# Four layers of graph attention on one core: layer 3's row totals from weights added up in pairs on VectorE

## The chip, the core and the metric

The kernel runs on one core of a Trainium2 chip. A core has five engines, each with an instruction stream of its own that it works through in order: TensorE (PE: matrix products and transposes, results in PSUM), VectorE (DVE), ScalarE (ACT), GpSimd (POOL) and SyncE (SP, which issues transfers). [...] The metric is the time of one execution on the device in microseconds (us), the median of the runs.

## The reference, cut to what matters

Sixteen batches of 1024 nodes with 256 features go through four layers of graph attention. Each layer begins with a normalisation and a relu and adds its result to x.

```python
h = jnp.maximum(_layernorm(x, axis=-1), 0.0)      # (x - mean) / sqrt(var), then relu
x = x + _L3_gnn_ref(h, adj, ...)                  # layers 0, 1, 2 in the same way

def _L3_gnn_ref(nodes_embed, node_adj, W, a_src, a_dst, bias, ln_gamma, ln_beta):
    h = jnp.einsum('bnd,hde->bhne', nodes_embed, W)            # H=4 heads of 64 features
    ...                                  # weight[i,j] = e_src[i] + e_dst[j] where there is an edge
    weight = jax.nn.leaky_relu(weight, negative_slope=0.01)
    weight = jnp.where(node_adj[:, None] == 0, NEG, weight)
    attention = jax.nn.softmax(weight, axis=-1)
    dst = jnp.einsum('bhij,bhje->bhie', attention, h) + bias[None, :, None, :]
    out = jax.nn.relu(dst) + h
    ...                                  # each head is normalised over its 64 features
```

A softmax is a sum of weights times values, divided by the total of the weights. The kernel makes the exponentials as products of one factor for the target i and one for the source j, so a weight is the larger (or smaller) of two such products, times the mask. Common factors of i cancel in the quotient. In layer 3 a factor q[j] is kept out of the weights and lies in the values: the values are q[j] h[j], and the total is the sum over j of q[j] w[j,i].

## The kernel before

The source nodes j lie in NI = 8 blocks of 128 on the partitions, the 1024 targets in the free dimension. Weights are made on VectorE, one instruction for one block of sources, from a row in PSUM (the same on all partitions), a factor of j for each partition and the mask:

```python
def weigh(b, turn, c, op, into):
    while row_taken:                    # one row in PSUM, shared by the two streams
        yield 0.25
    row_taken.append(b)
    r = psum.tile([P, N], F32, name="row", bufs=1)
    for i in range(NI):
        turn(r[:, ts(i, P)], i)         # TensorE makes the row
    yield 0.5
    for j in range(NI):
        w = edges.tile([P, N], F32, name=f"weights{b % 2}")      # 8 buffers for each stream
        nc.vector.scalar_tensor_tensor(w, r, c(j), masks[b][:, j // 2, :, j % 2], op0=op, op1=ALU.mult)
        into.append(w)
        ...
        yield 0.5
```

Layers 0 to 2 take their products from these weights as 128x257 matmuls (values and total together, L461). In layer 3 a head has only 64 features, and the weights are the moving operand: four matmuls of 32 columns, one on each quarter of the array, run side by side as a group.

```python
def in_tiles(parts, accT, first, last):
    for n, (values, moving) in enumerate(parts):
        ...
        made = nc.tensor.matmul(accT[ts(n, QUAD), :], values, moving, start=first, stop=last)   # L586

def add_values(h, j):                   # 2 groups of four: blocks j+1 and j
    for n in (j + 1, j):
        parts = [(V3[:, n, h, ts(e, QUAD)], moving) for moving in halves_of(h, n) for e in range(2)]
        in_tiles(parts, acc, n == 3, n == NI - 4)

def add_totals(h, j):                   # 1 group of four for the two blocks
    parts = [
        (V3[:, j + n, h, E:].to_broadcast([P, QUAD]), halves_of(h, j + n)[g])
        for g, n in ((0, 1), (0, 0), (1, 1), (1, 0))
    ]
    in_tiles(parts, total, j == 2, j == NI - 4)

for h in range(H):
    acc, total = accumulator(b), accumulator(b)
    ...                                 # head 0: the values first, then a transpose for the rows of heads 1 to 3
    behind = weigh3(h + 1)              # the next head's weights are made behind this head's products
    yield from start(behind, b)
    for first in range(0, NI, 4):       # a chunk is four blocks
        pinned = []
        for j in (first + 2, first):
            add_totals(h, j)
            if h > 0:
                add_values(h, j)
        for _ in range(4):
            next(behind, None)
        yield 1.8 if h == 0 else 5.4
    ...                                 # copies of acc and total, transposes, division, bias, relu, normalisation
```

Before each layer's projection two blocks of x are centered and cut at zero, on VectorE, and their squares are summed on ScalarE:

```python
def center_by_sums(xb, minus_mean, pair, centered):
    for n in range(2):
        nc.vector.tensor_scalar(                                 # L302
            centered[:, n, :], xb[:, 2 * pair + n, :], minus_mean[:, n : n + 1], 0.0,
            op0=ALU.add, op1=ALU.max,
        )
    ...
```

Two streams, of the even and the odd batches, are interleaved. A generator yields a virtual length for each of its steps, the stream that is behind goes on, and stream 1 starts LAG = 111 later, so that layer 3 of one stream is issued beside earlier layers of the other:

```python
streams = [[0.0, stream(0)], [LAG, stream(1)]]
while streams:
    ahead = min(streams, key=lambda s: s[0])
    t = next(ahead[1], None)
    ...
    ahead[0] += t
```

Of the kernel before, what the change touches and what calls it, by code (L numbers as in the profile page):

```python
# [32 lines left out]
F32 = mybir.dt.float32  # L33
BF = mybir.dt.bfloat16
# [4 lines left out]
ALU = mybir.AluOpType  # L39
# [22 lines left out]
def short_path(ctx: ExitStack, tc: tile.TileContext, ins: dict, out: bass.AP, bad: bass.AP):  # L62
# [233 lines left out]
    def accumulator(b: int) -> bass.AP:  # L296
        return psum.tile([P, HALF], F32, name=f"acc{b % 2}")

    def center_by_sums(xb: bass.AP, minus_mean: bass.AP, pair: int, centered: bass.AP) -> bass.AP:

        for n in range(2):
            nc.vector.tensor_scalar(  # L302
                centered[:, n, :], xb[:, 2 * pair + n, :], minus_mean[:, n : n + 1], 0.0,
                op0=ALU.add, op1=ALU.max,
            )
        squared = small.tile([P, 2], F32, name="squared")
        for n in range(2):
            square = work.tile([P, D], BF, name="square", bufs=1)
            nc.scalar.activation(  # L309
                square, xb[:, 2 * pair + n, :], AF.Square, bias=minus_mean[:, n : n + 1],  # L310
                accum_out=squared[:, n : n + 1],
            )
        return inverse_root(squared, 2, D, LN_EPS)

    def project(b: int, l: int, xb: bass.AP, sums: bass.AP, pair: int, evict):


        centered = work.tile([P, 2, D], F32, name="centered", bufs=3)
        if sums is None:
            mv = small.tile([P, 2, nc.vector.BN_AGGR_DIM], F32, name="mv", bufs=2)  # L320
            for n in range(2):
                stats = small.tile([P, nc.vector.BN_STATS_DIM], F32, name="stats", bufs=1)
                nc.vector.bn_stats(stats, xb[:, 2 * pair + n, :])
                nc.vector.bn_aggr(mv[:, n, :], stats)
                nc.vector.tensor_scalar(  # L325
                    centered[:, n, :], xb[:, 2 * pair + n, :], mv[:, n, 0:1], 0.0,
                    op0=ALU.subtract, op1=ALU.max,
                )
            rstd = inverse_root(mv[:, :, 1], 2, D, LN_EPS, D)
        else:  # L330
            minus_mean = small.tile([P, 2], F32, name="minus_mean")
            nc.vector.tensor_scalar_mul(minus_mean, sums[:, ts(pair, 2)], -1.0 / D)  # L332
            rstd = center_by_sums(xb, minus_mean, pair, centered)
        yield 0.5
        turned = psum.tile([P, NK, 2 * P], F32, name="misc")
        for n in range(2):
            for k in range(NK):
                nc.tensor.transpose(turned[:, k, ts(n, P)], centered[:, n, ts(k, P)], ident)  # L338
        hT = wide.tile([P, NK, 2 * P], F32, name="hT", bufs=3)
        nc.scalar.mul(hT, turned, ROOT_D)  # L340
        yield 1.0
        for n in range(2):
            projected = accumulator(b)[:, : D + EXT[l]]
            for k in range(NK):
                nc.tensor.matmul(  # L345
                    projected, hT[:, k, ts(n, P)], W[l][:, k, :],
                    start=(k == 0), stop=(k == NK - 1),
                )
            evict(2 * pair + n, projected, rstd[:, n : n + 1])
        yield 2.5  # L350
# [50 lines left out]
    def batch(b: int):  # L401
# [130 lines left out]


        h3, ex = last["h3"], last["ex"]
        y = single.tile([P, NI, H, E], F32, name="y")
        normed = []

        def center(h: int, blocks=slice(0, NI), engine=nc.gpsimd):
# [19 lines left out]
        def rescale(yh: bass.AP, blocks, head, rstd: bass.AP, engine=nc.gpsimd):  # L558
            shape = list(yh.shape)
            nc.vector.tensor_mul(yh, yh, rstd.unsqueeze(2).to_broadcast(shape))  # L560
            engine.tensor_mul(yh, yh, gamma[:, head].unsqueeze(1).to_broadcast(shape))
            engine.tensor_add(yh, yh, xb[:, blocks, head])

        weights = []

# [37 lines left out]
                ]  # L603
                in_tiles(parts, acc, n == 3, n == NI - 4)

        def add_totals(h: int, j: int):

            parts = [
                (V3[:, j + n, h, E:].to_broadcast([P, QUAD]), halves_of(h, j + n)[g])
                for g, n in ((0, 1), (0, 0), (1, 1), (1, 0))  # L610
            ]
            in_tiles(parts, total, j == 2, j == NI - 4)

        behind = weigh3(0)
        yield from start(behind, b)

        rest = small.tile([P, NI, H], F32, name="rest", bufs=1)
        nc.gpsimd.tensor_scalar_mul(rest, ex[:, :, 2 * H :], THIRDS)
# [2 lines left out]
        nc.gpsimd.tensor_sub(rest, rest, thirds[:, 0])  # L621
        nc.gpsimd.tensor_copy(thirds[:, 1], rest)
        nc.gpsimd.tensor_sub(thirds[:, 2], rest, thirds[:, 1])
        for h in range(H):


            acc = accumulator(b)
            total = accumulator(b)
            if h == 0:
                for first in range(0, NI, 4):  # L630
                    for _ in range(4):
                        next(behind)
                    pinned = []
                    for j in (first + 2, first):
                        add_values(h, j)
                    yield 3.6
                for _ in behind:
                    pass
                turned_thirds = psum.tile([3 * QUAD, P], BF, name="misc")
                made = nc.tensor.transpose(  # L640
                    turned_thirds, thirds.rearrange("p t i h -> p (t i h)"), ident_bf
                )
                tc.keep_in_program_order(made)
                thirds_T = small.tile([3 * QUAD, P], BF, name="thirds_T", bufs=1)
                nc.scalar.copy(thirds_T, turned_thirds)
            behind = weigh3(h + 1)
            yield from start(behind, b)

            for first in range(0, NI, 4):
                pinned = []  # L650
                for j in (first + 2, first):
                    add_totals(h, j)
                    if h > 0:
                        add_values(h, j)
                for _ in range(4):
                    next(behind, None)
                yield 1.8 if h == 0 else 5.4
            for _ in behind:
                pass
            copies = []  # L660
            for accT in (acc, total) if h == 0 else (total, acc):
                copies.append(wide.tile([P, HALF], F32, name="sums"))
                nc.scalar.copy(copies[-1], accT)  # L663
                next(testing)
                next(coming, None)
            sums, totals = copies if h == 0 else copies[::-1]
            yield 0.5
            turned = psum.tile([P, NG, P], F32, name="misc")
            for i in range(NG):
# [14 lines left out]
                inv.unsqueeze(3).to_broadcast([P, NH, NG, E]),  # L684
            )
            yield 0.5
            if h > 0:
                rescale(*normed.pop())


# [2 lines left out]
            elif h < H - 1:  # L693
                normed.append(center(h, engine=nc.gpsimd if h < H - 2 else nc.vector))
            else:
                normed += [center(h, slice(g * NG, g * NG + NG), nc.vector) for g in range(NH)]
            yield 1.0
        for _ in coming:
            pass
        while normed:  # L700
            rescale(*normed.pop(0), engine=nc.vector if len(normed) == 0 and b == B - 1 else nc.gpsimd)
        for g in range(NH):
            queue = nc.gpsimd if b < B - 1 else (nc.sync, nc.scalar)[g]
            queue.dma_start(
                in_blocks(out[b, ts(g, HALF), :]),
                y[:, ts(g, NG)].rearrange("p (c t) h e -> p c t (h e)", t=2),
            )
        yield 1.0

# [395 lines left out]
```

## Time and profile before

The median is 2933.43 us (three runs, 2932.9 to 2933.43). The profiled execution has a span of 2931.4 us with a granted TensorE clock of 0.995.

| group (line, engine) | count | busy us | mean ns |
|---|---|---|---|
| L461 TensorE, products of layers 0 to 2 | 6144 records | 1435.6 | 384 |
| L586 TensorE, layer 3's values and totals | 6144 records | 691.7 | 596 |
| L345 TensorE, projections | 2048 records | 516.1 | 389 |
| L367 VectorE, weights of layer 3 | 512 | 629.0 | 1272 |
| L367 VectorE, weights of layers 0 to 2 | 384 | 473.7 | 1273 |
| L302 VectorE, relu(x - mean) | 504 | 195.7 | 416 |
| L393 ScalarE, exponential of 128x256 | 256 | 121.1 | 473 |

An fp32 matmul leaves two records, so 6144 records are 3072 matmuls. The four matmuls of a group run side by side, so the busy time of L586 is less than the sum of its records. A busy share is the mean over the whole span. Windows split the span into stretches and give each engine's busy time in each. A line that a group of instructions has in the profile is the line of the helper that issues them.

### The profile page before, as it was taken

Reading aid. Unit: us, or ns where it says so; the run is one execution under the profiler, and the core shown is the slowest. Engines: PE = TensorE matmul, PEld = TensorE weight load, DVE = VectorE, ACT = ScalarE, POOL = GpSimd, SP = SyncE. Lnnn points to the kernel's source line nnn. Section 1 sums busy time; section 2 is a strip of 40 time slices with the busy share of each in tenths; the row PEclk is TensorE's granted clock in tenths of the full one; section 3 lists DMA queues with packets and bytes.
Section 4 is the critical chain, followed back from the end, with each engine's and each line's share of the span. In section 5 each row is a group of like instructions: output and inputs, shape, how many; then the busy total and the mean of one; then the engine's idle time right before and its main releaser. Section 6 shows DMA issues by size and latency. Waiting matters only on the chain.

```text
span 2931.4 us, 44756 instructions
## 1 busy us (share of the span) xinstructions
PE 2810.0 (96%) x16790; PEld 1961.9 (67%) x16790; DVE 2147.9 (73%) x4490; ACT 1088.2 (37%) x3010; POOL 981.3 (33%) x1533
## 2 busy tenths in 40 slices
PE   7999999999999999999999999999999999999986
PEld 5775857668576685766758577685766857667552
DVE  5658688586976859778586885868768587685857
ACT  1333434343343433424334343433434334343332
POOL 2123324243242423424233242432424224242333
PEclk9999999999999999999999999999999999999998
DMA  8204022030321303122031220303203031110101
GB/s 126 39 8 65 30 30 58 8 51 29 37 51 16 56 17 51 37 29 59 1 51 37 30 58 8 51 30 37 51 12 47 29 49 39 15 30 1 22 22 31
DMA packets 127967, 106.14 MB, mean 36 GB/s; under 512 B 79872, under 2 KB 98432, under 8 KB 127744
## 3 DMA queue, kind: packets, MB, share of 16 engines
q0 software_dynamic: 47328, 66.10, 15.4%
q1 hardware_dynamic: 79568, 35.53, 5.4%
q8 instruction: 135, 2.21, 0.3%
q10 hardware_dynamic: 848, 1.57, 0.2%
q14 instruction: 88, 0.72, 0.1%
HBM read 153.49 MB, written 33.55 MB: 64 GB/s over the span
## 4 chain that ended last, share of the span: by engine, by line
PE 59%; DVE 26%; issue 8%; POOL 3%; ACT 3%; DMA 0%; POOLq 0%; ACTq 0%; SPq 0%; DVEq 0%
PE acc L461 36%; DVE weights L367 16%; PE acc L586 10%; PE acc L345 9%; PE misc L338 2%; DVE centered L302 2%; POOL rstd L293 2%; DVE V L417 1%; PE row L374 1%; POOL y L544 1%; DVE y L545 1%; DVE var L555 1%; ACT square L309 1%; DVE y L551 1%; DVE mean L549 1%
## 5 line engine op out<-in xcount | busy, mean ns | idle before, releaser
L461 PE MATMUL acc<-V,weights 128*128 128x257 f32 x6144 | 1435.6, 384 | 33.5 <-DVE weights L367 15.7
L461 PEld LDWEIGHTS acc<-V,weights 128*128 128x128 f32 x6144 | 1136.6, 190 | 281.9 <-DVE weights L367 75.3
L586 PE MATMUL acc<-weights,V 128*32 128x512 f32 x6144 | 691.7, 596 | 12.0 <-DVE weights L367 8.1
L367 DVE SCALAR_TENSOR_TENSOR weights<-row,ex,mask 128x1024 f32<-128x1024 f32 x512 | 629.0, 1272 | 97.3 <-PE row L574 65.8
L345 PE MATMUL acc<-W,hT 128*128 128x259 f32 (+1 forms) x2048 | 516.1, 389 | 38.1 <-ACT hT L340 26.9
L367 DVE SCALAR_TENSOR_TENSOR weights<-row,V,mask 128x1024 f32<-128x1024 f32 x384 | 473.7, 1273 | 0.8 <-PE row L374 0.8
L345 PEld LDWEIGHTS acc<-W,hT 128*128 128x128 f32 x2048 | 378.7, 190 | 135.1 <-ACT hT L340 44.4
L586 PEld LDWEIGHTS acc<-weights,V 128*32 128x32 f32 x6144 | 189.1, 110 | 417.7 <-issue 410.3
L393 ACT ACTIVATE below<-acc,inv 128x256 f32<-128x256 f32 x256 | 121.1, 473 | 813.1 <-DVE inv L386 569.6
L293 POOL TENSOR_TENSOR rstd<-rstd,minus_half 128x2 f32<-128x2 f32 (+1 forms) x321 | 292.8, 912 | 20.3
L309 ACT ACTIVATE square<-x_b,minus_mean 128x256 bf16<-128x256 f32 x504 | 255.7, 507 | 110.3 <-DVE minus_mean L332 105.3
L441 POOL TENSOR_TENSOR x_b<-x_b,beta 128x256 f32<-128x256 f32 x128 | 93.5, 731 | 488.6 <-ACT square L309 483.5
L292 POOL TENSOR_SCALAR rstd<-squared 128x2 f32<-128x2 f32 x252 | 80.0, 317 | 464.0 <-ACT square L309 451.0
L385 DVE TENSOR_SCALAR inv<-acc 128x1 f32<-128x1 f32 x256 | 39.1, 153 | 255.3 <-PE acc L461 254.0
L302 DVE TENSOR_SCALAR centered<-x_b,minus_mean 128x256 f32<-128x256 f32 x504 | 195.7, 416 | 5.1
L340 ACT ACTIVATE hT<-misc 128x512 f32<-128x512 f32 x256 | 150.2, 592 | 129.6 <-PE misc L338 129.3
L396 DVE SCALAR_TENSOR_TENSOR x_b<-below,x_b 128x256 f32<-128x256 f32 x256 | 131.8, 515 | 84.9 <-ACT below L393 83.0
L663 ACT COPY sums<-acc 128x512 f32<-128x512 f32 x128 | 74.9, 585 | 308.6 <-PE acc L586 301.0
L413 ACT ACTIVATE V<-acc,rstd 128x3 f32<-128x3 f32 x384 | 98.4, 261 | 231.1 <-PE acc L345 230.6
L417 DVE TENSOR_SCALAR V<-acc,rstd,V 128x256 f32<-128x256 f32 x256 | 131.4, 537 | 59.8 <-ACT V L413 58.9
L338 PE MATMUL misc<-ident,centered 128*128 128x128 f32 x1024 | 158.7, 277 | 13.7 <-DVE centered L325 11.5
L170 POOL DMA_DIRECT2D adj_i<-in_adj_dram x128 | 74.4, 582 | 290.1 <-ACT adj_i L175 248.8
(96 smaller groups left out, 2212.8 us busy)
## 6 DMA issues: line engine op xcount, KB each, us to landing
adj_i<-in_adj_dram POOLq DMA_DIRECT2D x128, 256.0 KB, 3.9
x_b<-in_x_dram SPq DMA_DIRECT2D x15, 1024.0 KB, 6.4
narrow<-in_adj_dram POOLq DMA_DIRECT2D x60, 256.0 KB, 9.3
out_dram<-y POOLq DMA_DIRECT2D x30, 512.0 KB, 7.5
x_b<-in_x_dram ACTq DMA_DIRECT2D x4, 256.0 KB, 6.1
narrow_half<-in_adj_dram POOLq DMA_DIRECT2D x4, 256.0 KB, 16.9
mask<-narrow SPq DMA_TRANSPOSE x60, 3.7
weights<-in_L_gnn_a_dram SPq DMA_DIRECT2D x3, 256.0 KB, 5.5
```

What stands on the lines that cost most here:

```text
L293: nc.gpsimd.tensor_tensor(r, r, minus_half.to_broadcast([P, n]), op=ALU.pow)
L302: nc.vector.tensor_scalar(centered[:, n, :], xb[:, 2 * pair + n, :], minus_mean[:, n : n + 1], 0.0, op0=ALU.add, op1=ALU.max,)
L309: nc.scalar.activation(square, xb[:, 2 * pair + n, :], AF.Square, bias=minus_mean[:, n : n + 1], accum_out=squared[:, n : n + 1],)
L338: nc.tensor.transpose(turned[:, k, ts(n, P)], centered[:, n, ts(k, P)], ident)
L340: nc.scalar.mul(hT, turned, ROOT_D)
L345: nc.tensor.matmul(projected, hT[:, k, ts(n, P)], W[l][:, k, :], start=(k == 0), stop=(k == NK - 1),)
L367: nc.vector.scalar_tensor_tensor(w, r, c(j), masks[b][:, j // 2, :, j % 2], op0=op, op1=ALU.mult)
L393: nc.scalar.activation(below, acc[:, :D], AF.Exp, scale=inv)
L396: nc.vector.scalar_tensor_tensor(xi, below, 1.0, xi, op0=ALU.min, op1=ALU.add)
L417: nc.vector.tensor_scalar(V[:, i, :D], projected[:, :D], rstd, V[:, i, D : D + 1], op0=ALU.mult, op1=ALU.mult,)
L461: nc.tensor.matmul(accs[i], weights[j][:, ts(i, P)], V[:, j, : D + 1], start=(j == 0), stop=(j == NI - 1),)
L586: made = nc.tensor.matmul(accT[ts(n, QUAD), :], values, moving, start=first, stop=last)
```

## The change

The total of a head needs, for two neighbouring blocks j and j+1, q[j] w[j] + q[j+1] w[j+1]. The change has VectorE make s = (q[j] / q[j+1]) w[j] + w[j+1] first, and TensorE then takes s times q[j+1]: one matmul for each half of the targets instead of two. It is for TensorE, which has the largest busy share. The tiles of the totals come a chunk after those of the values, so that TensorE need not wait for the sums that VectorE makes from the newest weights. With that the end of a head (`close`) moves into the next head's first chunk. The relu(x - mean) of layers 1 to 3 goes from VectorE to ScalarE. The head's result y lies in V3 now, and the final sum in x_b, which frees the space of the tile y; the two buffers of the sums are new.

```diff
         for n in range(2):
-            nc.vector.tensor_scalar(
-                centered[:, n, :], xb[:, 2 * pair + n, :], minus_mean[:, n : n + 1], 0.0,
-                op0=ALU.add, op1=ALU.max,
-            )
+            x_n, mean_n = xb[:, 2 * pair + n, :], minus_mean[:, n : n + 1]
+            if l > 0:
+                nc.scalar.activation(centered[:, n, :], x_n, AF.Relu, bias=mean_n)
+            else:
+                nc.vector.tensor_scalar(
+                    centered[:, n, :], x_n, mean_n, 0.0, op0=ALU.add, op1=ALU.max
+                )
 ... (cut)
-        y = single.tile([P, NI, H, E], F32, name="y")
+        y = V3[:, :, :, :E]
 ... (cut)
-            engine.tensor_add(yh, yh, xb[:, blocks, head])
+            engine.tensor_add(xb[:, blocks, head], yh, xb[:, blocks, head])
 ... (cut)
-        def add_totals(h: int, j: int):
+        def add_totals(h: int, first: int):
             parts = [
-                (V3[:, j + n, h, E:].to_broadcast([P, QUAD]), halves_of(h, j + n)[g])
-                for g, n in ((0, 1), (0, 0), (1, 1), (1, 0))
+                (
+                    V3[:, first + 2 * n + 1, h, E:].to_broadcast([P, QUAD]),
+                    added[h, first, n][:, ts(g, HALF)],
+                )
+                for g in range(NH)
+                for n in range(2)
             ]
-            in_tiles(parts, total, j == 2, j == NI - 4)
+            in_tiles(parts, totals_of[h], first == 0, first > 0)
+
+        def add_up(h: int, first: int):
+            for n in range(2):
+                s = added[h, first, n] = single.tile([P, N], F32, name="added", bufs=2)
+                j = first + 2 * n
+                w, w1 = weights[h * NI + j], weights[h * NI + j + 1]
+                nc.vector.scalar_tensor_tensor(
+                    s, w, ratio[:, j + 1, h : h + 1], w1, op0=ALU.mult, op1=ALU.add
+                )
 ... (cut)
+        ratio = ex[:, :, :H]
+        nc.vector.reciprocal(ratio, ratio)
+        nc.gpsimd.tensor_mul(ratio[:, 1:], ratio[:, 1:], V3[:, : NI - 1, :, E])
 ... (cut: the old loop over heads; its end becomes close(h, sums))
+        for h in range(H):
+            acc = accumulator(b)
+            if h > 0:
+                behind = weigh3(h + 1)
+                yield from start(behind, b)
+            for first in range(0, NI, 4):
+                if h == 0:
+                    for _ in range(4):
+                        next(behind)
+                pinned = []
+                for j in (first + 2, first):
+                    add_values(h, j)
+                if first > 0:
+                    totals_of[h] = accumulator(b)
+                if to_add:
+                    add_totals(*to_add.pop())          # the chunk before
+                if first == 0 and h > 0:
+                    closing = close(*to_close)         # the head before
+                add_up(h, first)
+                to_add.append((h, first))
+                if h > 0:
+                    for _ in range(4):
+                        next(behind, None)
+                    yield 2.7
+                    yield from closing
+                    closing = iter(())
+                    yield 2.0
+                else:
+                    yield 3.6
 ... (cut: head 0's transpose and head 1's weights; the last totals and close after the loop)
```

## The prediction

> **What bounds the kernel now.** I read the page's busy shares first, then the costliest groups, then busy time by windows over one steady batch, and last the order in which each engine's instructions stand in the kernel before and in the changed one (that order holds no times).
>
> ```profile
> PE 2810.0 (96%) x16790; PEld 1961.9 (67%) x16790; DVE 2147.9 (73%) x4490; ACT 1088.2 (37%) x3010; POOL 981.3 (33%) x1533
> ...
> L586 PE MATMUL acc<-weights,V 128*32 128x512 f32 x6144 | 691.7, 596 | 12.0 <-DVE weights L367 8.1
> L367 DVE SCALAR_TENSOR_TENSOR weights<-row,ex,mask 128x1024 f32<-128x1024 f32 x512 | 629.0, 1272 | 97.3 <-PE row L574 65.8
> ...
> L302 DVE TENSOR_SCALAR centered<-x_b,minus_mean 128x256 f32<-128x256 f32 x504 | 195.7, 416 | 5.1
> ```
>
> TensorE is busy 96% of the span; layer 3's tiles (L586) are a quarter of that, and a third of those tiles are the totals that the change halves. VectorE has 73%, which looks like room. But that is a mean. The timeline of TensorE repeats every 178.5 us, one period for each batch, and the windows over one period give:
>
> ```profile
> 1004.00:1094.00 90.00, 87.48 (x432) 74.25 (x431) 57.77 (x150) 37.01 (x115) 32.85 (x60) 1.00 0.10 30
> 1094.00:1174.00 80.00, 78.53 (x561) 43.89 (x563) 72.39 (x120) 26.01 (x65) 23.02 (x29) 1.00 0.35 47
> 1174.00:1182.50 8.50, 8.50 (x64) 4.33 (x57) 3.26 (x7) 5.16 (x10) 5.67 (x6) 1.00 0.09 6
> ```
>
> After the length, the columns are PE, PEld, DVE, ACT and POOL busy. The second window is layer 3 of one batch beside layers 1 and 2 of the other stream. There VectorE is busy 72.4 of 80 us (90%) and TensorE 78.5. So TensorE bounds all three windows, but in layer 3 VectorE is only some 7 us behind it. The reader is to see that the change takes TensorE work and adds VectorE work in the very window where both are nearly full.
>
> ```profile
> L396 DVE SCALAR_TENSOR_TENSOR x_b<-below,x_b x256: 407/424/1525, 82.3 to 2841.2; 128x256 f32<-128x256 f32 x128
> ```
>
> ```profile
> L545 DVE SCALAR_TENSOR_TENSOR y<-y,h x65: 410/691/1654, 226.3 to 2916.9; 128x512 f32<-128x512 f32 x63, 128x256 f32<-128x256 f32 x2
> ```
>
> ```profile
> 1100.49 5.36 PE L586 MATMUL acc<-weights,V 128*32 128x512 f32 x48
> ```
>
> ```profile
> 1106.44 9.62 DVE L367 SCALAR_TENSOR_TENSOR weights<-row,ex,mask 128x1024 f32<-128x1024 f32 x8 [3.87 <-PE row L574]
> ```
>
> The first two (one tile's instructions each, min/median/max ns) are VectorE instructions with two SBUF tensors, the kind that the change adds. The other two are from the timelines of TensorE and VectorE: 48 tile records every 5.29 us (0.110 us each, two records to a matmul, so 0.88 us for a group of four tiles), and 8 weights in 9.62 us, so 1.20 us from one to the next.
>
> **What the Trainium skill says.** "VectorE: DVE Perf Modes", the section on the TRN2 errata, gives an fp32 operation of two tensors (N+151)/0.96 ns. For N=512 that is 691 ns, and the trace's median is 691 (L545). For N=1024 it makes 1224 ns: my estimate for one added-up pair, 1.12 to 1.14 us from start to start, as such instructions overlap by about 0.08 us in the timeline. "SBUF — State Buffer", the section Who interferes with whom, says that a VectorE instruction with two SBUF inputs is blocked by a GpSimd instruction that reads SBUF, for all of its length. The trace fits: L396 has a median of 424 ns, a mean of 515 and a maximum of 1525. "Perfetto Trace Analysis", Optimization Strategy, says that the most contended engine can change from regime to regime; the windows above are close to that.
>
> **The change part by part.**
>
> *TensorE.* A head now has 2 groups of totals tiles and not 4. That is 8 groups fewer per batch, 8 x 0.88 = 7.05 us of 178.5; 16 batches, 113 us. If nothing else moved, 2820 us.
>
> *VectorE, added.* 4 pairs per head and 4 heads: 16 x 1.12 = 18 us per batch, plus a reciprocal of 0.2.
>
> *VectorE, taken away.* relu(x - mean) of layers 1 to 3: 24 per batch x 0.416 = 10 us. But the order of instructions shows only 6 of 32 relus in the layer-3 stretch of before (0.36 us each from start to start, 2.2 us); the others lie where VectorE had room. Net for the batch +8 us (133 to 141), for layer 3 about +16.
>
> *ScalarE.* 24 more instructions of about 0.47 us (as L393): 11 us per batch, 68 to 79 of 178. No bound; it does put a ScalarE step between the mean and the transposes.
>
> *Moved.* A head's totals, copies and rescaling come a chunk into the next head; y lies in V, and the result goes into x_b. The counts stay the same. The batch's virtual length in the interleaving falls (layer 3's sum of yields from 51.2 to 47.0) while LAG stays at 111, and in the changed order the two streams no longer alternate evenly: between equal points of successive batches TensorE has 150.0 and 182.2 us of work by turns, where it had 173.2 each time. The sum of two is 332.2 for 346.4, the 14.1 us saved.
>
> *Running sums over layer 3.* I start both engines at the row of head 0, from which its weights follow at once, and add up each engine's instructions in order, with the start-to-start times above (0.43 us per 128x257 matmul, 0.46 per projection matmul, 0.13 per transpose; VectorE 1.20 weights, 1.12 pair, 0.43 and 0.47 for the two ELU adds, 0.61 for each 128x512 of the normalisation). Before: the last weights of head 3 are made after 67.3 us of VectorE work, and TensorE first wants that chunk after 80.5 us: 13 us of room. After, in one stream (A): the last pair of head 3 is made after 76.9 us and wanted after 69.9; the other stream's next weights, behind it, come after 92.6 and are wanted from 81.0. The shortage is 11.6 us. In the other stream (B): the second pair of head 3 comes after 68.8 us, and its tiles stand at 54.4: 14.4 us. (B's last pair stands at 89.2 against 77.5.) B's 89.2 us are 32 weights 38.4, 16 pairs 17.9, 8 weights of the other stream 9.6, normalisation 11, the rest ELU, sums and evictions. After the stretch TensorE is the bound again and in order, so it cannot make the time up.
>
> *The sum for two batches.* -14.1 saved, +11.6 +14.4 TensorE waiting for VectorE, -2.8 for waits of before in these stretches that are swallowed (L461's 0.6 and 0.5 us and the like). That gives +9. Two terms more: the pairs have two buffers for one chunk, so a pair waits for the tiles of the chunk before. In B's head 0 VectorE stands at 12.8 us, and those tiles end at 15 plus the 3 us that TensorE is already late: 5 us lost on VectorE, which then comes later for all that follows. And GpSimd is busy 23 of 80 us in the stretch: 16 pairs x about 0.1 us as for L396, 2 us per batch, 4 for two. With both, +18 for two batches. Some seven steady pairs of batches give +63 to +127. The last batch has layer 3 alone, where VectorE is already as full as TensorE (weights at 1.28 with the normalisation between them): 12 to 16 pairs, +15. So 2933 + 78 to 2933 + 142 us; I take 3045.
>
> **The rivals.**
>
> 1. *TensorE stays the bound*, and most of the 113 us comes through: about 2830 to 2860. For it: 96% against 73% (after, 167 us against 141 per batch), and the tiles of the totals come a chunk later, which gives VectorE a chunk of time. Against it: the room is in the wrong window, and the weights of the next head are behind the pairs in VectorE's order, so that lateness is passed on to the values.
>
> 2. *A draw:* VectorE bounds layer 3, but gives back just the gain, 2900 to 2980. This needs shortages of 7 us and not 12 to 14, say by pairs of about 0.8 us. Nothing in the trace has such a rate for two fp32 tensors.
>
> 3. *ScalarE's relu becomes a wait of its own* in the projections: L338 would wait on ScalarE. Its queue there already shows waits of 1.7 us (L345 for L340, once a period). Some 1 to 2 us per batch, 15 to 30 us more. Possible, not in my centre.
>
> **Range and chances.** The low end, 2985, is the sum without buffers and ports, and with a third of the shortage absorbed; the high end, 3105, is all terms. Slower by over 2% (above 2992) 0.84; within 2% 0.10; faster by over 2% 0.06, for the case that my running sums misread how the order plays out.
>
> **What would show it.** Right: TensorE busy falls to about 2700 us and its share below 92%; VectorE at about 2300; waits of layer-3 tiles (now 12 us on VectorE) and of the transposed rows go to 100 us and more, named by weights and pairs; layer-3 windows with VectorE at 95% and over; periods of two batches near 370 us and not 357; mean of a pair 1.25 us or more. Wrong: steady pairs of batches near 345 us with VectorE's gaps left in layer 3, pairs well below 1.1 us, or lost time that stands before transposes and projections.

## The result, and the profile after

The changed kernel takes 3227.66 us (median of four runs, 3226.99 to 3228.16) against 2933.43 before: 1.1003 times, interval 1.0984 to 1.1022. The range on record ended at 3105. Lines have moved by about five: L592 is L586 of before (layer 3's tiles), L372 is L367 (weights), L466 is L461 (products of layers 0 to 2), L350 is L345 (projections), L390 and L391 are L385 and L386 (the inverse of a total). L632 makes a pair, L306 is the relu on ScalarE.

Busy shares and groups of the changed kernel, as before:

```profile
PE 2852.8 (88%) x15766; PEld 1958.8 (61%) x15766; DVE 2331.0 (72%) x4378; ACT 1245.8 (39%) x3394; POOL 1043.3 (32%) x1549
...
L592 PE MATMUL acc<-weights,V 128*32 128x512 f32 x4096 | 514.3, 647 | 121.3 <-DVE weights L372 89.0
...
L632 DVE SCALAR_TENSOR_TENSOR added<-weights,ex,weights 128x1024 f32<-128x1024 f32 x256 | 334.1, 1324 | 63.6 <-PE acc L592 63.6
L306 ACT ACTIVATE centered<-x_b,minus_mean 128x256 f32<-128x256 f32 x384 | 177.4, 504 | 450.0 <-DVE minus_mean L337 449.3
...
L592 PE MATMUL acc<-added,V 128*32 128x512 f32 x1024 | 161.5, 598 | 21.1 <-DVE added L632 21.1
```

TensorE lost 1024 matmul records and is nevertheless 42.8 us busier than before (2810.0). That is the line to stop at: less work, more busy time. One record of a tile of layer 3 has a mean of 647 ns, where it had 596. Idle time of TensorE went from 121.4 us (2931.4 less 2810.0) to 373.5.

The two streams no longer alternate evenly, so the unit is a pair of batches. First the windows of the changed kernel over one steady pair: layer 3 of one stream, the stretch behind it, layer 3 of the other, the stretch behind that.

```profile
817.80:898.40 80.60, 73.62 (x503) 36.64 (x501) 76.64 (x119) 32.21 (x80) 24.61 (x26) 0.96 0.20 33
898.40:986.40 88.00, 78.84 (x376) 64.57 (x377) 52.26 (x125) 39.86 (x117) 35.39 (x64) 0.98 0.11 31
986.40:1084.20 97.80, 84.40 (x545) 45.38 (x545) 88.59 (x126) 27.74 (x66) 30.25 (x30) 0.97 0.30 41
1084.20:1210.30 126.10, 117.31 (x556) 97.13 (x553) 72.14 (x172) 56.29 (x164) 40.70 (x73) 0.97 0.16 28
sum 392.50, PE 354.17 PEld 243.72 DVE 289.63 ACT 156.10 POOL 130.95; mean PE 354.17 PEld 243.72 DVE 289.63 ACT 156.10 POOL 130.95
```

and a pair of the kernel before:

```profile
1100.35:1457.40 357.05, 349.06 (x2100) 244.93 (x2098) 266.80 (x553) 136.43 (x378) 123.06 (x190) 1.00 0.21 36
```

VectorE is busy 95% and 91% of the two layer-3 windows; there it has become the bound. But look at the column behind POOL, the granted clock: 0.96 to 0.98 in every window, where it was 1.00. A pair takes 35.5 us more. Idle TensorE time rose from 8.0 to 38.3, which is 30.3. Its busy time should have fallen by the 14.1 saved and rose by 5.1: 19.2 us more than the work in it. 30.3 + 19.2 - 14.1 is the 35.5 (35.4 by the rounded terms).

What TensorE waits for in that pair of the changed kernel (total, times, longest, us):

```profile
PE acc L592 <- DVE weights L372: 9.2, 4, 3.4
PE acc L466 <- DVE weights L372: 6.2, 5, 2.8
PE misc L665 <- ACT sums L654: 4.3, 2, 3.2
PE acc L592 <- DVE inv L391: 4.1, 1, 4.1
PE acc L350 <- ACT hT L345: 3.2, 4, 1.4
PE acc L350 <- ACT V L420: 3.1, 2, 2.7
PE acc L592 <- DVE added L632: 2.1, 2, 1.5
```

With smaller ones, 25.2 us are put down to VectorE (2.4 before) and 12.0 to ScalarE (4.7 before). The pairs themselves (`added`) are only 2.1: what is missed is mostly what stands behind them. The clock is seen in TensorE's timeline:

```profile
1050.95 5.26 PE L592 MATMUL acc<-weights,V 128*32 128x512 f32 x32 [4.06 <-DVE inv L391]
1056.02 1.02 PE L592 MATMUL acc<-added,V 128*32 128x512 f32 x2
...
1058.53 1.06 PE L592 MATMUL acc<-added,V 128*32 128x512 f32 x6 [1.49 <-DVE added L632]
...
1071.24 3.64 PE L592 MATMUL acc<-weights,V 128*32 128x512 f32 x32
...
1276.60 2.09 PE L350 MATMUL acc<-W,hT 128*128 128x259 f32 x4 [2.65 <-ACT V L420]
1278.62 5.77 PE L592 MATMUL acc<-weights,V 128*32 128x512 f32 x32
```

The columns are start, length, and in brackets the idle time ahead. The same 32 records of tiles take 3.64 us undisturbed, 5.26 after a wait of 4.06 us and 5.77 after one of 2.65 us. The four projection records ahead of the last take 2.09 where others take 1.04. The granted clock's record is at one half from 1050.85 on for 3.4 us and from 1276.1 on for 6.8 us. The Trainium skill, "TensorE: Matmul & The Clock Gate", Part 1, the section What's actually happening, says that TensorE's clock falls to a half after an idle window of about 3.4 us, is full again after about 3.4 us of sustained work, and that this window runs free of the kernel. The trace agrees on the half, on stretches of 3.4 and 6.8 us, and on the free window: all 46 stretches of this run begin on one grid of 3.413 us. It differs on the onset, as 2.65 us of idle time were enough here. Also at 1056.02: a group of four tiles whose second pair is late is cut, and a single matmul (two records) takes 1.02 us, as long as the whole group of four.

Two chains behind these waits. First the 4.06 us, in VectorE's timeline of the same kernel (L632 makes pairs, L372 weights):

```profile
1043.10 2.47 DVE L632 SCALAR_TENSOR_TENSOR added<-weights,ex,weights 128x1024 f32<-128x1024 f32 x2
1045.49 0.22 DVE L390 TENSOR_SCALAR inv<-acc 128x1 f32<-128x1 f32 x2
1045.95 4.86 DVE L372 SCALAR_TENSOR_TENSOR weights<-row,ex,mask 128x1024 f32<-128x1024 f32 x4 [0.24 <-PE row L580]
1050.72 0.21 DVE L391 RECIPROCAL inv<-inv 128x1 f32<-128x1 f32 x2
```

The wait is put down to `inv`, which ends last ahead of it. But by the order of the instructions these tiles take the last of the four weights first, and that one ends at 1050.81, 0.14 us before they start. The pairs and the tiles' own weights stand in one queue, 2.5 us of pairs ahead: this is the lateness that was predicted. Second the 2.65 us, in ScalarE's timeline:

```profile
1275.39 0.64 ACT L559 ACTIVATE wide<-V 128x512 f32<-128x512 f32 x1 [1.57 <-DVE V L557]
...
1276.08 0.46 ACT L420 ACTIVATE V<-acc,rstd 128x256 f32<-128x256 f32 x1
```

The copy that frees the accumulator (L420) stands on ScalarE behind a step of the normalisation (L559), which waits for VectorE. ScalarE is 39% busy; it passes VectorE's lateness on, by its order. Such waits were not in my sums.

### The profile page after: what moved, and what is told of

It is laid out like the page before. It is cut to its first block, busy times and chain, and to the rows that moved or that the text cites. A ratio compares the mean times of both kernels' runs of the same rounds, so it can differ in the third digit from the quotient of the medians.

```text
span 3226.3 us, 42751 instructions
## 1 busy us (share of the span) xinstructions
PE 2852.8 (88%) x15766; PEld 1958.8 (61%) x15766; DVE 2331.0 (72%) x4378; ACT 1245.8 (39%) x3394; POOL 1043.3 (32%) x1549
## 5 line engine op out<-in xcount | busy, mean ns | idle before, releaser
L466 PE MATMUL acc<-V,weights 128*128 128x257 f32 x6144 | 1454.3, 387 | 62.6 <-DVE weights L372 48.6
L466 PEld LDWEIGHTS acc<-V,weights 128*128 128x128 f32 x6144 | 1138.1, 191 | 326.4 <-DVE weights L372 122.1
L372 DVE SCALAR_TENSOR_TENSOR weights<-row,ex,mask 128x1024 f32<-128x1024 f32 x512 | 628.3, 1275 | 8.2 <-PE row L379 6.1
L592 PE MATMUL acc<-weights,V 128*32 128x512 f32 x4096 | 514.3, 647 | 121.3 <-DVE weights L372 89.0
L350 PE MATMUL acc<-W,hT 128*128 128x259 f32 (+1 forms) x2048 | 543.0, 403 | 77.8 <-ACT hT L345 31.3
L350 PEld LDWEIGHTS acc<-W,hT 128*128 128x128 f32 x2048 | 381.8, 196 | 200.5 <-ACT hT L345 54.3
L372 DVE SCALAR_TENSOR_TENSOR weights<-row,V,mask 128x1024 f32<-128x1024 f32 x384 | 469.2, 1275 | 20.2 <-PE row L379 19.8
L592 PEld LDWEIGHTS acc<-weights,V 128*32 128x32 f32 x4096 | 134.0, 117 | 435.1 <-issue 389.3
L632 DVE SCALAR_TENSOR_TENSOR added<-weights,ex,weights 128x1024 f32<-128x1024 f32 x256 | 334.1, 1324 | 63.6 <-PE acc L592 63.6
L306 ACT ACTIVATE centered<-x_b,minus_mean 128x256 f32<-128x256 f32 x384 | 177.4, 504 | 450.0 <-DVE minus_mean L337 449.3
L293 POOL TENSOR_TENSOR rstd<-rstd,minus_half 128x2 f32<-128x2 f32 (+1 forms) x321 | 319.7, 996 | 20.1
L292 POOL TENSOR_SCALAR rstd<-squared 128x2 f32<-128x2 f32 x252 | 66.8, 265 | 598.5 <-ACT square L314 586.3
L170 POOL DMA_DIRECT2D adj_i<-in_adj_dram x128 | 76.5, 598 | 525.5 <-ACT adj_i L175 405.8
L390 DVE TENSOR_SCALAR inv<-acc 128x1 f32<-128x1 f32 x256 | 37.7, 154 | 247.5 <-PE acc L466 246.2
L345 ACT ACTIVATE hT<-misc 128x512 f32<-128x512 f32 x256 | 150.1, 595 | 100.9 <-PE misc L343 100.4
L343 PE MATMUL misc<-ident,centered 128*128 128x128 f32 x1024 | 165.9, 282 | 17.7 <-DVE centered L330 11.3
L592 PE MATMUL acc<-added,V 128*32 128x512 f32 x1024 | 161.5, 598 | 21.1 <-DVE added L632 21.1
```

The costliest lines, as they stand in the source:

```text
L293: nc.gpsimd.tensor_tensor(r, r, minus_half.to_broadcast([P, n]), op=ALU.pow)
L306: nc.scalar.activation(centered[:, n, :], x_n, AF.Relu, bias=mean_n)
L350: nc.tensor.matmul(projected, hT[:, k, ts(n, P)], W[l][:, k, :], start=(k == 0), stop=(k == NK - 1),)
L466: nc.tensor.matmul(accs[i], weights[j][:, ts(i, P)], V[:, j, : D + 1], start=(j == 0), stop=(j == NI - 1),)
L632: nc.vector.scalar_tensor_tensor(s, w, ratio[:, j + 1, h : h + 1], w1, op0=ALU.mult, op1=ALU.add)
```

## The experiments

Each is timed against the kernel before, run beside it. "Pair" is the period of one steady pair of batches, read as above; idle is what of it TensorE is not busy; half is the time in it at half clock.

| run | median us | ratio (95% interval) | pair | idle | half |
|---|---|---|---|---|---|
| before | 2933.43 | 1 | 357.0 | 8.0 | 0 |
| after | 3227.66 | 1.1003 (1.0984 to 1.1022) | 392.5 | 38.3 | 23.9 |
| y in V alone | 2931.09 | 0.9991 (0.9982 to 0.9999) | 356.7 | 7.7 | 0 |
| y in V, relu on ScalarE | 3005.34 | 1.0247 (1.0230 to 1.0264) | 365.6 | 14.1 | 3.4 |
| y in V, unread pairs | 3126.21 | 1.0657 (1.0640 to 1.0675) | 381.3 | 25.7 | 20.5 |
| after, narrow pairs | 3051.73 | 1.0403 (1.0385 to 1.0420) | 372.1 | 26.2 | 20.5 |
| after, relu on VectorE | 3295.45 | 1.1234 (1.1216 to 1.1253) | 402.9 | 43.0 | 34.1 |
| order alone | 3063.13 | 1.0441 (1.0426 to 1.0457) | 373.1 | 26.6 | 17.1 |
| old order, narrow pairs | 2964.26 | 1.0103 (1.0088 to 1.0119) | 359.1 | 17.4 | 0 |
| old order, full pairs | 3121.74 | 1.0642 (1.0626 to 1.0658) | 380.0 | 31.6 | 10.2 |
| after, LAG 109 | 3303.93 | 1.1262 (1.1245 to 1.1279) | 405.8 | 48.7 | 58.0 |
| pairs in head 3 alone | 2981.32 | 1.0165 (1.0151 to 1.0179) | 362.3 | 13.7 | 0 |
| two pairs a batch | 3003.34 | 1.0239 (1.0225 to 1.0253) | 365.4 | 16.2 | 3.4 |
| two pairs, late | 2982.04 | 1.0166 (1.0152 to 1.0179) | 361.1 | 13.6 | 0 |
| two pairs, behind the ELU | 2940.22 | 1.0022 (1.0014 to 1.0030) | 357.2 | 9.0 | 0 |
| after, ratio in its own tile | 3226.26 | 1.0995 (1.0978 to 1.1011) | 392.0 | 39.2 | 20.5 |
| order alone, ratio in its own tile | 3062.33 | 1.0432 (1.0416 to 1.0448) | 373.1 | 26.7 | 17.1 |

The steady pairs of batches of one run are alike within 1.4%, but their time at half clock is not: it is 13.7 to 20.5 us with unread pairs, 23.9 to 37.5 for the change with the relu on VectorE, 44.4 to 58.0 at LAG 109, and 0 to 10.2 for two pairs, late. It is 0 in every steady pair of batches for the old order with narrow pairs.

### The pairs' size: narrow pairs in the changed kernel

A pair is added over 128 of its 1024 columns; the rest of the sum is left out (the tiles read a constant there), and the order stays that of the change.

```diff
-                    s, w, ratio[:, j + 1, h : h + 1], w1, op0=ALU.mult, op1=ALU.add
+                    s[:, :P], w[:, :P], ratio[:, j + 1, h : h + 1], w1[:, :P],
+                    op0=ALU.mult, op1=ALU.add,
```

> The changed kernel with each pair added up over 128 of the 1024 columns only (the rest of the two tiles holds ones, so the totals are incomplete); every tile, lag and the relu on ScalarE stay. Theory A (VectorE is short in layer 3 because of 16 pairs of 1.3 us per batch, and the waits halve TensorE's clock): nearly all waits on weights and pairs go, clock back to 0.99, 2800 to 2860 us. Rival B (the new order, the lag of the totals and the end of a head in the next head's first chunk cost the time): above 3100. Rival C (relu on ScalarE as a wait): above 3050.

3051.73 us: theory A is missed by far, B too, and only the figure of C is met, by 2 us. The cut in the pairs' length is worth 176 us of the 294. A narrow pair still has a mean of 464 ns, where a full one has 1324, so the other 118 us hold a third of the pairs' time; the rest is not their length.

### The relu back on VectorE

```diff
-            if l > 0:
+            if l > 3:
```

> The changed kernel with relu(x - mean) of layers 1 to 3 back on VectorE. Theory A: VectorE has 10 us more per batch, 1.5 to 2.5 us of it in layer 3, the rest where it has room: 3230 to 3290 us. Rival C (ScalarE's relu holds up the projections): 3130 or less.

3295.45 us, 68 more and 5 above the range of theory A. In the changed kernel ScalarE's relu is a help and no cost; rival C falls.

### y and relu alone, y alone

The kernel before with y in V, and with or without the relu on ScalarE.

```diff
-        y = single.tile([P, NI, H, E], F32, name="y")
+        y = V3[:, :, :, :E]
```

> The kernel before with only two parts of the change: relu(x - mean) of layers 1 to 3 on ScalarE, and y in V with the result in x_b. No pairs, the totals as before. Theory A: these parts cost almost nothing, 2915 to 2960 us. Rival C: 3000 or more.

> The kernel before with y in V and the result in x_b, nothing else. If relu on ScalarE made the 72 us of the run that had both: 2925 to 2945 us. If y in V made them: 2990 or more.

y in V is free (2931.09), so the relu costs 74 us in the order of before, though ScalarE is only 41% busy; theory A is missed, C's figure is met. Where it costs, the waits of TensorE over the whole span show:

```profile
PE acc L350 <- ACT above L400: 32.0, 36, 2.2
PE acc L350 <- DVE V L422: 23.5, 14, 1.7
PE misc L343 <- ACT hT L345: 20.4, 14, 1.5
```

Before, the first two are 5.4 and 5.3. The projections wait for accumulators that ScalarE's ELU and VectorE's copy release late. The third, transposes that wait for ScalarE, is what rival three named, but it is no growth: the projections' own wait for `hT` fell from 26.9 to 3.0 us.

### Pairs that nobody reads

y in V, and 16 pairs a batch behind their chunk's products in the order of before; TensorE's work is that of before.

```diff
+                for n in range(2):
+                    j = first + 2 * n
+                    unread = single.tile([P, N], F32, name="unread", bufs=2)
+                    nc.vector.scalar_tensor_tensor(
+                        unread, weights[h * NI + j], ex[:, j + 1, H + h : H + h + 1],
+                        weights[h * NI + j + 1], op0=ALU.mult, op1=ALU.add,
+                    )
```

> The kernel before with y in V (for the room), all its own tiles for the totals, and beside them the change's 16 pairs per batch added up on VectorE, which nothing reads. TensorE keeps its 7 us per batch that the change takes away; nothing waits for a pair, only for the weights behind it. Theory A: running sums leave VectorE 9 us short per batch (48.8 us of work against 39.4 at the weights of head 2), with port contention 10 to 12 us: 3080 to 3150 us, with the slow clock on top at most 3200; so it is faster than the changed kernel although it does more work on TensorE. Rival B (the order, not the load): 2930 to 2980.

3126.21, as theory A had it: VectorE's load in this place costs 195 us over y in V, with no pair on TensorE's path. The wait is for what stands behind it, weights that follow two unread pairs directly (once more put down to the `inv` behind them), and the clock follows:

```profile
1390.94 6.64 PE L586 MATMUL acc<-weights,V 128*32 128x512 f32 x48 [5.86 <-DVE inv L386]
```

48 records take 6.64 us where the kernel before has 5.36.

### The clock

I set each wait of TensorE, from 300 us to some 80 or 90 us before the end, beside the clock's record (its times counted from the span's first instruction), and counted a wait when a half-clock stretch begins in it or within 4 us after.

| run | waits | with half clock |
|---|---|---|
| before | 97, all but one below 2.5 us | 2 |
| after, below 2.5 us | 161 | 18 |
| after, 2.5 us and more | 45 | 38 |
| order alone, 3 us and more | 27 | 27 |
| unread pairs, 4.5 us and more | 14 | 14, 7.8 us each |
| LAG 109, 4.5 us and more | 28 | 28, 7.3 us each |

The bounds of the rows differ, and a wait's length alone does not decide: in the changed kernel all 15 waits of 2.5 to 3 us brought half clock, and only 23 of the 30 that were longer. One that did not:

```profile
1008.41 3.64 PE L592 MATMUL acc<-weights,V 128*32 128x512 f32 x32 [3.36 <-DVE weights L372]
```

The grid of 3.413 us accounts for it. One of its borders, 1006.48, splits these 3.36 us into 1.4 and 1.9, while the 2.65 us ahead of 1276.60 have 2.2 on one side. Over the changed kernel, up to its last 100 us, 41 windows of the grid ran at full clock with 2.0 us or more of idle TensorE, and half clock followed 39 of them; it followed 2 of the 469 with less. In all 17 runs together the border is less sharp: 323 of 357 from 2.0 us on, 62 of 211 from 1.6 to 2.0, 4 of 7148 below.

So such a wait is paid for twice. Of the 23.9 us at half clock TensorE is busy in 20.8, which costs at most 10.4 of the 19.2 us. Another 4.9 are the tiles of the pairs, none of them at half clock:

```profile
817.80:1210.30 392.50, 19.98 (x128) 0.97 0.19 33
```

This is TensorE's busy time on the tiles of `added` in that pair of batches. From start to start the 16 groups take 19.0 us, where 0.88 each makes 14.1: three are cut in two (0.97 more each), and a group that stands alone takes 0.97 as well. Some 4 us are left. The products of layers 0 to 2 and the projections are 7.2 us longer, with at most 3.2 from the clock; why, I did not trace.

### The order by itself

Narrow pairs and relu on VectorE: what is left of the change is its order, and the TensorE work that it saves. Then the same narrow pairs, and full ones, in the order of before (no lag of a chunk, no moved close).

```diff
-                for j in (first + 2, first):
-                    add_totals(h, j)
-                    if h > 0:
+                if h > 0:
+                    for j in (first + 2, first):
                         add_values(h, j)
+                add_pairs(h, first)
```

> The changed kernel with narrow pairs (128 of 1024 columns) and relu of layers 1 to 3 back on VectorE: what is left of the change is its order (totals a chunk behind, the end of a head in the next head, the two streams unevenly apart) and the shorter TensorE work. With narrow pairs alone it was 3052. Theory D (relu on ScalarE and the order add up, each a cost of its own): the 4.3 us per batch that relu and y cost in the kernel before come off, 2970 to 3010 us. Theory A as first put (only VectorE's load counts): VectorE is now loaded more by 10 us per batch, 3052 or more. If the order cost nothing: 2830 to 2860.

> The kernel before with y in V and the totals of all heads from narrow pairs (128 of 1024 columns, totals incomplete), in its own order: the totals in their own chunk, the end of a head at its end, relu on VectorE. TensorE has the change's 7 us less per batch, VectorE hardly more. Theory D (in the run with the changed order and narrow pairs, 3063 us, it is the order that costs): 2820 to 2870 us. If TensorE's gain can't be had in any order (small groups of tiles, splits): 2920 or more.

> The same with full pairs: the change's pairs in the order of the kernel before, each chunk's totals behind its values. Running sums: VectorE 16.1 us short per batch (74.5 us of work against 58.4). 178.5 - 7 + 16 + 2 and some 6 us of slow clock: 3090 to 3230 us. If the chunk of lag in the changed kernel helps as intended: above 3230. If the lag and the moved end of a head do harm: below 3180.

The order alone makes 3063.13, though 14.1 us of tiles a pair fall away. Theory D is missed; the first form of theory A has the figure, but narrow pairs in the old order, with the same load on VectorE, make 2964.26. With full pairs, and the relu on VectorE in both, the old order has 3121.74 and the new one 3295.45. So the new order, which was to spare TensorE a wait, costs 99 and 174 us. The lag, the moved close and the shorter yields that came with them were not taken apart.

Narrow pairs in the old order are still 31 us slower than before, with no half clock in the pair of batches:

```profile
1293.41:1652.54 359.13, 341.73 (x1971) 241.07 (x1970) 274.17 (x587) 136.91 (x378) 121.29 (x192) 1.00 0.22 36
```

TensorE's busy time falls by 7.3 us and not by 14.1, mostly since the tiles of the pairs take 19.3 from start to start here too, and its idle time grows by 9.4: theory D is missed here as well, and the saving in tiles was not had whole in either order. With full pairs 10.2 us of a pair of batches run at half clock in the old order, 34.1 in the new.

### Even streams

LAG is 109 instead of 111, so that successive batches have nearly equal periods (201 to 204 us, but for the last).

> The changed kernel with LAG 109 and not 111, so that both streams again come at equal distances. Rival E (the uneven distance of the streams is what costs): 3120 us or less. Theory A: the running sums leave VectorE 15.3 us short per batch, where the uneven order has 11.6 and 14.4 by turns; 3200 to 3280 us.

3303.93 us, a miss: worse by 76. Uneven streams are not the fault. The waits here are fewer and longer, and 44 to 58 us of a pair run at half clock.

### Pairs in the last head alone

I took VectorE to have room in head 3, for which no next head's weights are made. Four pairs a batch there, then two (chunk 0 of head 3, tiles at the head's end), in the order of before with y in V.

```diff
+                if h == H - 1:
+                    add_pairs(h, first)
```

```diff
+                if h == H - 1 and first == 0:
+                    pairs = add_up(h)
...
+                if h == H - 1 and first > 0:
+                    in_tiles(pairs, total, False, True)
```

> The kernel before with y in V, and pairs in head 3 only, its totals after its values in each chunk; heads 0 to 2 and relu as before. TensorE loses two groups of tiles per batch, 1.8 us; VectorE has 4 pairs more, where the running sums leave it 13 us of room behind the last weights of head 3 (last pair made at 70.8 us, wanted at 70.3). Theory A (load where there is room costs nothing): 2900 to 2918 us. If any pair on VectorE costs more than its tiles on TensorE: 2945 to 2990.

> The kernel before with y in V and only two pairs per batch: chunk 0 of head 3, their tiles at the end of the head, behind all others, so that no group waits for them. TensorE 0.9 us less per batch, VectorE 2.3 us more where the running sums leave it 11 us of room. If room on VectorE can be used at all: 2912 to 2926 us, against 2931 with y in V alone. If VectorE's order makes even these cost: 2935 to 2960.

2981.32, as the second theory had it (a pair costs more than its tiles save), and 3003.34, above both ranges. Two pairs a batch (3.5 us on VectorE, at a mean of 1747 ns) cost 72 us over y in V, 4.5 a batch.

### The reciprocal's wait

In the changed kernel the reciprocal of `ex` is made in place and waits for GpSimd, which still reads `ex` (34.3 us in nine waits). I took this for a cost that my sums had left out. Here it goes into a tile of its own, in the changed kernel and in its order alone.

```diff
-        ratio = ex[:, :, :H]
-        nc.vector.reciprocal(ratio, ratio)
+        ratio = small.tile([P, NI, H], F32, name="ratio", bufs=1)
+        nc.vector.reciprocal(ratio, ex[:, :, :H])
```

> The changed kernel, but the reciprocal for the pairs is not made in place: it goes into a tile of its own, so that it need not wait until GpSimd has read ex (in the changed kernel 4.4 us of VectorE time, once in two batches, with head 0's weights right behind it and 3.4 us of TensorE waiting, then tiles at half clock). Theory (this wait is a cost that my running sums left out, small beside the pairs themselves): 3150 to 3200 us, 4 to 9 us less for two batches. Rival (VectorE is behind by then anyway, the time is only lost later): 3215 us or more.

> The order of the change alone (narrow pairs, relu on VectorE, 3063 us) with the reciprocal in a tile of its own. Of this run's 26.6 us of idle TensorE time for two batches the pairs' load can explain little. Theory (the wait for GpSimd and the clock after it explain a third or more): 2990 to 3040 us. Rival (what is lost is the order itself: the moved close and the two streams' uneven work): 3050 us or more.

3226.26 and 3062.33: within 1.4 us of the in-place versions. That theory falls. What the reciprocal waits for in the run with its own tile:

```profile
  ACT ex L438: 25.2, 9
```

`ex` itself comes late; the wait has another name, and the weights behind it need `ex` too.

### The same two pairs at three places

First with the own ratio tile and made only behind the next chunk's weights. Then also tied by data to the inverse of the head before (plus 0 times that inverse), so that they must stand behind the other stream's ELU; the ratio itself is made earlier there.

```diff
+            if h == H - 2:
+                nc.vector.scalar_tensor_tensor(
+                    ratio[:, 1::2], inv[:, 0], 0.0, ratio[:, 1::2], op0=ALU.mult, op1=ALU.add
+                )
```

> The order of before with y in V and two full pairs for a batch (chunk 0 of head 3), as in the run of two pairs (3003 us), but the reciprocal has a tile of its own and the pairs stand on VectorE only after the weights of the chunk behind, with their tiles right behind. Theory (two pairs cost 68 us there through the in-place reciprocal's wait for GpSimd and through the other stream's ELU that stood behind the pairs): 2915 to 2950 us. Rival (any 2 us more on VectorE in layer 3 are passed on, wherever they stand): 2975 us or more.

> The two pairs for a batch again (chunk 0 of head 3, order of before, y in V), but tied by data to the inverse of the head before, so that on VectorE they stand behind the other stream's ELU and not in front of it (the ratio gets 0 times that inverse added, one 128x4 instruction). Same pairs, same tiles, the same 2.4 us of VectorE work for a batch. Theory (what two pairs cost is TensorE waiting for an accumulator that the ELU behind them releases, 3.1 us for a batch in the run of late pairs): 2910 to 2931 us, level with before or up to the 14 us of TensorE work that they save. Rival (any 2.4 us more on VectorE in layer 3 are passed on, wherever they stand): 2965 us or more.

Late: 2982.04 us, as the rival had it. VectorE's, GpSimd's and TensorE's timelines of that run:

```profile
1361.46 0.15 DVE L385 TENSOR_SCALAR inv<-acc 128x1 f32<-128x1 f32 x1
1361.53 1.27 DVE L623 SCALAR_TENSOR_TENSOR added<-weights,ratio,weights 128x1024 f32<-128x1024 f32 x1
1362.72 0.15 DVE L386 RECIPROCAL inv<-inv 128x1 f32<-128x1 f32 x1
1362.80 2.23 DVE L623 SCALAR_TENSOR_TENSOR added<-weights,ratio,weights 128x1024 f32<-128x1024 f32 x1
...
1367.48 0.16 DVE L386 RECIPROCAL inv<-inv 128x1 f32<-128x1 f32 x1
```

```profile
1361.62 2.32 POOL L561 TENSOR_TENSOR V<-V,gamma 128x512 f32<-128x512 f32 x1 [0.81 <-DVE inv L385]
```

```profile
1368.63 1.14 PE L345 MATMUL acc<-W,hT 128*128 128x259 f32 x4 [3.14 <-ACT above L395]
```

The pairs stand ahead of the reciprocals of two ELU blocks. ScalarE's `above` follows the second, and then the accumulator is free: TensorE waits 3.14 us for it, once a batch. The second pair takes 2.23 us, beside a GpSimd instruction of 2.32; so it does in all 16 batches (2.05 to 2.24). Behind the ELU: 2940.22 us, between theory and rival, 9 above the one and 25 below the other.

```profile
1348.13 0.16 DVE L386 RECIPROCAL inv<-inv 128x1 f32<-128x1 f32 x1
...
1350.52 1.27 DVE L626 SCALAR_TENSOR_TENSOR added<-weights,ratio,weights 128x1024 f32<-128x1024 f32 x1
...
1354.58 1.27 DVE L626 SCALAR_TENSOR_TENSOR added<-weights,ratio,weights 128x1024 f32<-128x1024 f32 x1
```

```profile
1349.28 1.14 PE L345 MATMUL acc<-W,hT 128*128 128x259 f32 x4 [0.42 <-ACT above L395]
```

The wait is 0.42, and all pairs but one take 1.27 or 1.28 us. The same pairs and tiles cost 51 us over y in V ahead of the ELU and 9 behind it, 2.6 us a batch apart. VectorE's time on the two pairs is 3.5 us a batch in the one place and 2.6 in the other, so 0.9 of the 2.6 can be the longer pair, which no run parts from what the pairs delay. For these two pairs the place, with what runs beside them there, is the cost, and not VectorE's fullness. The run stops short of a gain: TensorE's busy time of a pair of batches falls by 0.9 us and not by the 1.8 that two groups are worth, and its waits grow by 1.3. No version with pairs was faster than the kernel before. To place all 16 pairs in this way was not tried.

## Why the prediction failed in size

*The bound.* Right: VectorE took layer 3 over, at 95% and 91% of its windows, and the tiles' waits (121.3 and 21.1 us, from 12.0) are named by weights (89.0) and pairs (21.1). The unread pairs show VectorE's load, where the pairs stand, to be the larger cause. One of the signs of being wrong, lost time ahead of projections, shows in part: 8.6 us of a pair, where the kernel before has 4.4.

*The waits of TensorE.* 11.6 + 14.4 + 5 + 4 - 2.8 is 32 us a pair; measured 30.3 more idle. That the size fits is in part luck, as other waits are in it: 22.8 of the growth by the named releasers are VectorE's and 7.3 ScalarE's. The buffers' term holds: VectorE's pairs waited 7.5 us for tiles in that pair of batches, 4.9 of it at once, where 5 were taken. The running sums followed weights and pairs, and not the normalisation and the ELU on ScalarE, by which accumulators are held.

*TensorE's busy time: the step that failed.* The sum took 14.1 us a pair off and let every remaining instruction keep its duration, hence "about 2700" busy. It is 2852.8. Of the missing 19.2 us a pair up to 10.4 are the halved clock after waits, 4.9 the pairs' own tiles in cut and lone groups. Over seven pairs the 19.2 make 134 us, more than the loss predicted at the centre (112). It was the step *The sum for two batches* that had no term for it: 18 us a pair predicted, 35.4 measured, of which 19.2 are this and -1.9 the waits.

*The centre.* The full sum, +18 a pair, was put at the top of the range and the centre below; no term turned out to be absorbed. (The low end, 2985, absorbs a third of stream A's 11.6 us alone; a third of both shortages would make 2951.) With 18 for each of seven pairs and the 15 at the end it would have been 3075. Measured, seven pairs bring 246.

*The last batch.* +15 was too small. Its period went from 155.6 to 179.9 and what follows from 68.6 to 88.8: +44.5. The waits of that lone layer 3 are longer (17.7 us for weights), and the granted clock over its last 179 us is 0.83.

*Instruction costs.* A pair: median 1277 ns, mean 1324; predicted 1224 by the formula, 1.25 or more with ports. The excess of the mean over the median, 0.05 us for each of 16, is 0.8 us a batch, where 2 were taken. The relu on ScalarE has 504 ns for the 470 taken.

*Rivals.* One and two are out. Three was undersized and had the wrong sign: in the order of before the relu on ScalarE costs 74 us, not 15 to 30, but inside the change it saves 68.

*Open.* The clock's part is read from its record; no run holds the clock fixed. Why the change's order alone costs as much as it does is known by its waits (for weights 10.9 us a pair, for the copies of the values 4.7, for the sums 3.9) and not by one step; uneven streams and the in-place reciprocal were tested and are not it.

## What to carry to other kernels

Where an engine that bounds the kernel is made to wait, add to the wait what the clock costs after it: here tiles went from 3.64 to as much as 5.77 us after a wait of 2.65. Room on another engine is a matter of place: two pairs a batch cost 51 us ahead of a 0.2 us reciprocal that frees an accumulator, and 9 us behind it. So before adding work, list the short steps that it would delay and what each one releases, for every stream and not only for the one that is changed.

## What was not expected of the hardware

Half clock followed 39 of the 41 windows of the 3.413 us grid with 2.0 us or more of idle TensorE, and 2 of the 469 with less; so a wait of 2.65 us brought it and one of 3.36, split by a border, did not. A single tile matmul of a group of four takes as long as all four (1.02 against 1.04 us), so a group cut by a wait costs a group's time more. The weights kept their mean (1275 ns, 1272 before), while single pairs ran to 2306 ns; the late two show one pair of 2.23 us beside GpSimd in every batch.
